# The width-96 attention's output projection as seven products of block sums

## The chip, the core and the metric

The kernel runs on one core of one Trainium2 chip. The core has a matrix engine (TensorE, PE in the profile, with its weight loads on a row of their own, PEld), a vector engine (VectorE, DVE), a scalar engine (ScalarE, ACT), a general engine (GpSimd, POOL) and a queue engine from which this kernel issues all its DMAs (SyncE, SP). The metric is the time of one execution on the device in microseconds, and the time of a kernel is the median of its runs. Less is better.

## What is computed

A decoder of four layers on 1024 tokens (16 sequences of 64) of width 512. Each layer is a cross-attention over 64 context tokens per sequence and a feed-forward part, and both add their result to the stream `x`. The change touches layer 2's second part and layer 3:

```
# layer 2, second part: 64 experts of rank 16, gated by a top-16 router
h   = einsum('nd,krd->nkr', xf, A)
out = einsum('nkr,kdr->nd', h * G[:, :, None], B) * 2
# layer 3: 16 query heads in 4 groups, width 96; one key head for each group
q, k, v = latents @ Wq.T, hidden @ Wk.T, hidden @ Wv.T
out = softmax(q k / sqrt(96)) v          # 16 heads of 96: 1536 wide
x = x + out @ Wo.T                       # Wo: 1536 -> 512, in float32
# then a linear layer with 3-bit weights, and the end
```

## The kernel before

**Two lanes.** All tokens are 8 tiles of 128. From layer 1's second part on, the work is split into two lanes of 4 tiles each: lane b ("side", tiles 0 to 3) and lane a ("main", tiles 4 to 7). Each lane is a Python generator that traces instructions and yields a cost after each step; `merged` takes from the side lane as much cost as the main lane has just yielded, times a rate. That sets the order of TensorE's instructions, which is kept as written (`manual_schedule` for PE). The instructions of the other engines and of the DMA queue are ordered by the framework's scheduler from their readiness in its own simulation, and each queue then runs strictly in that order. When lane b's work ends, lane a goes on alone.

**Memory of weights.** Each lane has four pages of 128 x 2048 floats for weights (`Lane.page`). A page is handed to the next tile as soon as its last reader is done; a load that needs a page waits for that in the DMA queue.

**Products of block sums.** The expert layer (`lora_experts`) already multiplies two 2 x 2 block matrices with seven block products in place of eight (class `Seven`): `hidden` for the first factor, `output` for the second. The sums of the activations' blocks are made by GpSimd (`stream_sums`, `hidden_sums`), those of the weights' blocks once by GpSimd in `block_sums`, which runs beside lane b's layer-2 attention: for each of 8 parts of the weights it loads 512 KB, does four subtractions of 128x256 and stores 512 KB to device memory. Each part is then loaded by both lanes as 384 KB of blocks and 512 KB of sums (`LoraWeights.load`). `block_sums` advances by one step at each yield of lane b's layer-2 attention. Parts 0 to 3 of the expert layer lie in the lane's four pages, 4 and 5 in room of their own in the layer's pool, and 6 and 7 in the pages that come free after the first `hidden` half.

**Layer-3 attention** (`packed_attention`) has 8 units in a lane, (group, pair of tiles), in the order group by group. A software pipeline runs, in each iteration n, `keys` of unit n, `turn_weights` of unit n-2, `scores` of n-1, `queries` of n, `project_both` of n-3 and `values` of n-2. For a unit, `project_both` multiplies each of its two tiles by the group's rows of Wo: three chunks of 128 rows, 512 columns wide (`Attention.project`, line 746), and VectorE adds the result to `x` (line 159). The group's query and key weights and its rows of Wo take a page each (lines 1600 and 1601). After the last unit come the norms, the transposes and the products of the last linear layer (`Q3Linear`, line 1549).

A float32 product of the code stands as two records of TensorE in the profile: 4 groups x 4 pairs of tiles x 2 tiles x 3 chunks are 96 products, and the profile has x192.

Of the kernel before, what the change touches and what calls it, by code (L numbers as in the profile page):

```python
# [1290 lines left out]
class LoraWeights:  # L1291
# [5 lines left out]
    def load(self, n, room=None):  # L1297
        if n in self.parts:
            return
        w = self.ln.page("w_l2f", 7 * W2) if room is None else room  # L1300
        half = 3 * W2
        self.ln.nc.sync.dma_start(w[:, :half], self.src[n, :, :half])
        self.ln.nc.sync.dma_start(w[:, half:], self.kept[n])
        self.parts[n] = w


def lora_experts(ln, tiles, weights, w_r):


# [4 lines left out]
    with ExitStack() as es:  # L1314
# [3 lines left out]
        for n in range(4, 6):  # L1318
            weights.load(n, pool.tile([P, 7 * W2], F32, tag=f"w{n}", name="w_l2f", bufs=1))
# [38 lines left out]
        def stream_sums(p):  # L1358
            t, u = pairs[p]
            blocks = [k.kvT[:, c : c + 2, v, 1:3, :] for v in (t, u) for c in (0, 2)]  # L1360
            a11, a12, a21, a22 = blocks
            s = pool.tile([P, 4, 2, 2, S], F32, tag="s", name="sx", bufs=1)
            nc.gpsimd.tensor_tensor(s[:, 0], a21, a22, ALU.add)
            nc.gpsimd.tensor_tensor(s[:, 1], s[:, 0], a11, ALU.subtract)
            nc.gpsimd.tensor_tensor(s[:, 2], a11, a21, ALU.subtract)
            nc.gpsimd.tensor_tensor(s[:, 3], a12, s[:, 1], ALU.subtract)
            lhs[p] = {
                f"s{i + 1}": (lambda e, i=i: s[:, i, e].rearrange("p b s -> p (b s)"))
                for i in range(4)
            }  # L1370
            lhs[p]["a11"] = lambda e: k.stream(e, t)
            lhs[p]["a12"] = lambda e: k.stream(2 + e, t)
            lhs[p]["a22"] = lambda e: k.stream(2 + e, u)
# [64 lines left out]
        def output(p):  # L1438
            x = [k.x[v].rearrange("p (j n) -> p j n", j=2) for v in pairs[p]]

            def add(v, j, src):
                nc.vector.scalar_tensor_tensor(
                    x[v][:, j], src, SCALING, x[v][:, j], ALU.mult, ALU.add
                )

            m = Seven(ln, lhs.pop(p), [weights.parts[4 + e] for e in range(4)], "ps_o")
            s = pool.tile([P, 2, W2], F32, tag="u", name="uo")
            p1, p2 = m.products(2)
            nc.scalar.copy(s[:, 0], p1)
            add(0, 0, p1)  # L1450
            add(0, 0, p2)
            yield 3.45
            p6, p7 = m.products(2)
            nc.vector.tensor_tensor(s[:, 1], s[:, 0], p6, ALU.add)
            nc.vector.tensor_tensor(s[:, 0], s[:, 1], p7, ALU.add)
            yield 3.45
            p5, p4 = m.products(2)
            nc.vector.tensor_tensor(s[:, 1], s[:, 1], p5, ALU.add)
            add(1, 1, p5)
            add(1, 0, p4)  # L1460
            add(0, 1, s[:, 1])
            add(1, 1, s[:, 0])
            add(1, 0, s[:, 0])
            yield 3.45
            (p3,) = m.products(1)
            add(0, 1, p3)
            yield 1.7
# [15 lines left out]
        for n in range(6, 8):  # L1483
            weights.load(n)
        yield from turn(0, 1)
        hidden_sums(0)
        yield from hidden(1, 1)
        out = output(0)
        yield next(out)
        yield next(out)  # L1490
        yield from turn(1, 0)
        yield from turn(1, 1)
        hidden_sums(1)
        yield from out
# [3 lines left out]
class Q3Linear:  # L1498
# [6 lines left out]
    def load(self):  # L1505
        nc, ln = self.ln.nc, self.ln
        w_q, w_ranges, bias = self.src
        self.q3 = ln.page("w_l3f", NC * D).bitcast(I32)
        nc.sync.dma_start(self.q3, w_q)

        r = ln.page("r_l3f", NC * D).bitcast(F16)
        for g in range(4):
            nc.sync.dma_start(
                r[32 * g : 32 * (g + 1)], w_ranges[g].partition_broadcast(32)
            )
        self.r = r.rearrange("p (c j n) -> p c j n", c=NC, j=2)
        self.bias = self.pool.tile([P, D], F16, tag="b16", name="b16", bufs=1)
        nc.sync.dma_start(self.bias, bias.partition_broadcast(P))
        self.wT = ln.page("wT_l3f", NC * D).rearrange("p (c n) -> p c n", c=NC)
        self.kept = {}  # L1520

    def weights(self, c):
        nc = self.ln.nc
        w, low, high = self.wT[:, c, :], self.r[:, c, 0, :], self.r[:, c, 1, :]
        nc.vector.tensor_tensor(w, high, low, ALU.subtract)
        nc.vector.scalar_tensor_tensor(
            w, self.q3[:, c * D : (c + 1) * D], 1.0 / 7.0, w, ALU.mult, ALU.mult
        )
        nc.vector.tensor_tensor(w, w, low, ALU.add)
# [14 lines left out]
    def product(self, t):  # L1544
        ln, nc = self.ln, self.ln.nc
        xT = self.kept.pop(t)
        ps = ln.bank([P, D], "ps_o")
        for c in range(NC):
            nc.tensor.matmul(
                ps, lhsT=xT[:, c, :], rhs=self.wT[:, c, :], start=c == 0, stop=c == NC - 1  # L1550
            )
        ln.add_to(t, ps)
        nc.sync.dma_start(self.out[t * P : (t + 1) * P, :], ln.k.x[t])


def packed_attention(ln, tiles, w_in, w_v, last):
# [6 lines left out]
    with ExitStack() as es:  # L1563
# [31 lines left out]
        def head_weights(h):  # L1595
            if h < NKV and h not in heads:
                n_q, n_k = NC * G * HD, NC * P
                n = n_q + (n_k if h < NJ else 0)
                wa, wb = ln.page(f"l3a_w{h}", n), ln.page(f"l3a_o{h}", NJ * D)
                nc.sync.dma_start(wa, w_in[h, :, :n])  # L1600
                nc.sync.dma_start(wb, w_in[h, :, n_q + n_k :])
                heads[h] = (
                    wa[:, :n_q].rearrange("p (c n) -> p c n", c=NC),
                    wa[:, n_q:].rearrange("p (c n) -> p c n", c=NC) if h < NJ else None,
                    wb.rearrange("p (g n) -> p g n", g=NJ),
                )

        def keys(u):
            h, t = u
            if t == tiles[0]:  # L1610
                head_weights(h)
                head_weights(h + 1)
# [50 lines left out]
        def values(u):  # L1663
            h, t = u
            d = kept[u]
            aP = pool.tile([P, NJ, 4, S], F32, tag="aP", name="aP")
# [11 lines left out]
        def project(u, i):  # L1678
            h, t = u
            aP = kept[u]["aP"]  # L1680
            chunks = [
                aP[:, j, 2 * i : 2 * i + 2, :].rearrange("p b s -> p (b s)") for j in range(NJ)
            ]
            at.project(t + i, chunks, heads[h][2])

        def project_both(u):
            for i in range(2):
                project(u, i)

        linear = Q3Linear(ln, pool, *last)  # L1690
        units = [(h, t) for h in range(NKV) for t in tiles[::2]]
        for n in range(len(units) + 2):
            for lag, step, cost in [
# [4 lines left out]
                (3, project_both, 5.2),  # L1698
                (2, values, 1.7),
            ]:  # L1700
                if n == len(units) + 1 and step == project_both:

                    for c in range(2):
                        linear.weights(c)
                        yield 1.0
                if 0 <= n - lag < len(units):
                    own = step(units[n - lag])
                    yield cost if own is None else own
            if n == len(units):
                linear.load()  # L1710
# [8 lines left out]
        project(units[-1], 0)  # L1719
        yield 2.6  # L1720
        linear.norm(three)
        linear.turn(one)
        yield 0.5
        project(units[-1], 1)
        yield 2.6
        linear.norm(four)
        linear.turn(two)
        yield 0.5
        for t, ahead in zip(tiles, (three, four, None, None)):
            linear.product(t)  # L1730
            yield 3.4
            if ahead is not None:
                linear.turn(ahead)
                yield 0.5
# [44 lines left out]
def decoder_kernel(ctx: ExitStack, tc: tile.TileContext, i: dict, out: bass.AP):  # L1779
# [7 lines left out]
    kept_s = [kept.tile([P, 4 * W2], F32, tag=f"s{n}", name=f"sums_d{n}") for n in range(8)]  # L1787
# [46 lines left out]
    def last_layers(ln, tiles, weights):  # L1834
        yield from lora_experts(ln, tiles, weights, routers[0])
        yield from packed_attention(
            ln, tiles, i["l3a_w"], i["l3a_v"], [i["l3f_q"], i["l3f_r"], i["l3f_b"], out]
        )

    def side():  # L1840
# [7 lines left out]
        with ExitStack() as es:  # L1848
            sums = block_sums(b, b.pool(es, "sums"), i["l2f_w"], kept_s)
            weights = LoraWeights(b, i["l2f_w"], kept_s)  # L1850
            for cost in small_head_attention(b, halves[0], i["l2a_w"], weights):
                next(sums, None)
# [5 lines left out]
    def main():  # L1858
# [7 lines left out]
        weights = LoraWeights(a, i["l2f_w"], kept_s)  # L1866
# [10 lines left out]
def laid_out(a):  # L1877
# [63 lines left out]
    i["l2f_w"] = np.stack(parts + [blocks(w_b, e) for e in range(4)])  # L1941
    w = [a[f"L3_xattn_W{n}"].T for n in "qkvo"]
    i["l3a_w"] = per_head(w[0], w[1], None, w[3], 96, 4)
# [25 lines left out]
```

## Time and profile before

| | |
|---|---|
| time, median of 3 runs | 1618.26 us (1617.16 to 1623.63) |
| the profiled execution: time | 1624.97 us |
| its span, first to last instruction | 1622.9 us |
| mean granted TensorE clock | 0.989 |
| lane b's layer-2 attention | about 860 to 1040 us |
| lane b's expert layer and layer 3 | about 1040 to 1473 us |
| lane a's expert layer | about 1300 to 1411 us |
| lane a's layer 3 | about 1411 us to the end, alone from about 1473 us |
| the layer-3 Wo products (line 746, `l3a_o`) | 192 records, 85.5 us |
| GpSimd's sums of weight blocks (line 1252) | 32 instructions, 22.9 us |

How to read the profile: a table of busy time by engine comes first, then the span in 40 slices, then the chain of work that ended last, followed back from the last instruction. Rows of the chain are start, length, engine, tile written, line and number of records. In the groups of instructions a row is: line, engine, operation, tile written <- tiles read, shape, number; then the busy time in us and the mean length of one in ns; then the idle time of the engine ahead of them and what ended it. The mean length of a matmul record holds its latency, which overlaps the next one; the distance between the starts of neighbours is what a record costs.

### The profile page before, as it was taken

What the parts mean: (1) busy time and instruction counts of PE and PEld (TensorE: products, weight loads), DVE (VectorE), ACT (ScalarE), POOL (GpSimd) and SP (SyncE); (2) the same over time, 40 slices, a digit from 0 to 9 for tenths busy, and PEclk for the clock granted to TensorE, in tenths of its full rate; (3) what the DMA queues carried; (4) which work ended last, traced back from release to release, by engine and by line L of the source; (5) the groups of instructions that cost most, each with busy time, mean ns of one, the idle gap of its engine ahead of it and who ended that gap; (6) DMA issues with size and microseconds to landing.
All of it is one profiled execution on the core that took longest, in us unless ns stands there. A gap on an engine that the chain in (4) does not pass through costs nothing.

```text
span 1622.9 us, 21530 instructions
## 1 busy us (share of the span) xinstructions
PE 1564.4 (96%) x7291; PEld 950.1 (59%) x7296; DVE 994.2 (61%) x2084; ACT 621.5 (38%) x1944; POOL 578.4 (36%) x614
## 2 busy tenths in 40 slices
PE   7899899999999999999999999999999999999999
PEld 1234456465555645666665565667566578757774
DVE  6687587666687566777954465449345454622335
ACT  3333444244433444444443354321234433223442
POOL 2394237532286313853324433224122132111112
PEclk9999999999999999999999999999999999999999
DMA  8892349623695345944435622214220113201120
GB/s 233 269 288 88 115 145 266 193 83 102 191 271 159 108 142 168 272 156 176 170 129 206 230 76 92 79 46 179 72 69 21 36 73 128 64 26 46 39 72 26
DMA packets 104237, 215.06 MB, mean 133 GB/s; under 512 B 49600, under 2 KB 66752, under 8 KB 93504
## 3 DMA queue, kind: packets, MB, share of 16 engines
q1 hardware_dynamic: 104128, 213.68, 41.8%
q8 instruction: 59, 0.97, 0.2%
q14 instruction: 50, 0.41, 0.1%
HBM read 190.06 MB, written 23.59 MB: 132 GB/s over the span
## 4 chain that ended last, share of the span: by engine, by line
PE 77%; DVE 12%; DMA 4%; ACT 3%; POOL 2%; issue 2%; SPq 0%; ACTq 0%; POOLq 0%; DVEq 0%
PE ps_wo L746 15%; PE ps_q L860 10%; PE ps_kv L878 5%; PE ps_q L1636 5%; PE ps_ckv L812 5%; PE ps_a L737 4%; PE ps_s L696 4%; PE ps_pT L143 3%; PE ps_o L1279 3%; DMA att<-att_d 3%; PE ps_h L1279 3%; PE ps_v L1583 3%; PE ps_k L1620 3%; PE ps_wo L1206 2%; PE ps_q L1138 2%
## 5 line engine op out<-in xcount | busy, mean ns | idle before, releaser
L746 PE MATMUL ps_wo<-l1a_o,aT 128*128 128x512 f32 x512 | 233.6, 599 | 3.1 <-ACT aT L930 3.1
L860 PE MATMUL ps_q<-l1a_w,kvT 128*128 128x512 f32 x512 | 233.0, 598 | 0.0
L712 ACT ACTIVATE p<-ps_s,mx 128x128 f32<-128x128 f32 x384 | 135.4, 369 | 221.1 <-DVE mx L707 204.9
L721 POOL TENSOR_TENSOR p<-p,sm 128x512 f32<-128x512 f32 x96 | 103.7, 1081 | 301.2 <-DVE sm L720 270.5
L125 POOL TENSOR_TENSOR r<-r,mhalf 128x5 f32<-128x5 f32 (+1 forms) x96 | 101.9, 1062 | 222.6 <-DVE r L802 219.4
L860 PEld LDWEIGHTS ps_q<-l1a_w,kvT 128*128 128x128 f32 x512 | 96.3, 192 | 116.7 <-issue 115.2
L746 PEld LDWEIGHTS ps_wo<-l1a_o,aT 128*128 128x128 f32 x512 | 93.6, 192 | 101.5 <-issue 96.8
L159 DVE TENSOR_TENSOR x<-x,ps_wo 128x512 f32<-128x512 f32 x104 | 70.6, 679 | 112.5 <-PE ps_wo L746 78.4
L878 PE MATMUL ps_kv<-l1a_w,kvT 128*128 128x256 f32 x512 | 122.7, 383 | 2.7 <-DVE x L159 2.7
L478 POOL TENSOR_TENSOR acc<-acc,pv 128x512 f32<-128x512 f32 x96 | 121.5, 1291 | 4.4 <-DVE pv L468 3.7
L812 PE MATMUL ps_ckv<-l1a_kv,kvT 128*64 128x512 f32 x512 | 116.9, 598 | 4.4 <-ACT ckv L821 4.4
L801 DVE TENSOR_REDUCE r<-sq 128x5 f32<-128x640 f32 x64 | 52.3, 817 | 103.7 <-ACT sq L886 103.7
L878 PEld LDWEIGHTS ps_kv<-l1a_w,kvT 128*128 128x128 f32 x512 | 92.7, 191 | 19.1 <-DVE x L159 4.3
L868 ACT ACTIVATE sq<-ps_q 128x512 f32<-128x512 f32 x64 | 38.2, 598 | 151.4 <-PE ps_q L860 151.4
L468 DVE TENSOR_TENSOR pv<-att,ps_v 128x512 f32<-128x512 f32 x128 | 82.1, 677 | 22.4 <-DMA att<-att_d 17.8
L125 POOL TENSOR_TENSOR rs<-rs,mhalf 128x1 f32<-128x1 f32 x64 | 37.7, 595 | 162.4 <-DVE rs L134 157.9
L696 PE MATMUL ps_s<-kT,qT 128*128 128x128 f32 (+1 forms) x704 | 91.5, 275 | 0.0
L371 DVE TENSOR_TENSOR prod<-qs,kp 128x1024 f32<-128x1024 f32 x64 | 80.9, 1301 | 14.5 <-ACT qs L352 7.6
L696 PEld LDWEIGHTS ps_s<-kT,qT 128*128 128x128 f32 (+1 forms) x704 | 85.1, 192 | 2.3 <-issue 0.9
L1636 PE MATMUL ps_q<-kvT,l3a_w 128*128 128x256 f32 x384 | 85.5, 379 | 0.0
L746 PE MATMUL ps_wo<-l3a_o,aP 128*128 128x512 f32 x192 | 85.5, 593 | 0.0
L728 DVE COPY pT<-ps_pT 128x512 f32<-128x512 f32 x96 | 64.3, 682 | 31.3 <-PE ps_pT L143 31.1
(216 smaller groups left out, 2856.2 us busy)
## 6 DMA issues: line engine op xcount, KB each, us to landing
l1a_w<-in_l1a_w SPq DMA_DIRECT2D x32, 1536.0 KB, 7.3
att<-att_d SPq DMA_DIRECT2D x64, 512.0 KB, 9.3
l1a_o<-in_l1a_w SPq DMA_DIRECT2D x32, 1024.0 KB, 5.2
s<-ckv SPq DMA_DIRECT2D x32, 256.0 KB, 4.5
w_l2f<-sums_d SPq DMA_DIRECT2D x16, 512.0 KB, 5.5
w_l2f<-in_l2f_w SPq DMA_DIRECT2D x16, 384.0 KB, 4.3
l3a_w<-in_l3a_w SPq DMA_DIRECT2D x6, 1024.0 KB, 6.5
l3a_o<-in_l3a_w SPq DMA_DIRECT2D x8, 768.0 KB, 4.3
```

Of the source, the lines that this page charges most:

```text
L125: self.nc.gpsimd.tensor_tensor(out, v, self.k.mhalf[:, : v.shape[1]], ALU.pow)
L468: nc.vector.tensor_tensor(pv.rearrange("p (q w n) -> p q w n", w=2, n=L), att[:, a, :].rearrange("p (q w n) -> p q w n", w=2, n=L), spaced ...
L478: nc.gpsimd.tensor_tensor(sums, before, pv, ALU.add)
L696: nc.tensor.matmul(ps[:, i, :], lhsT=qT[:, i // 2, 2 * (i % 2) : 2 * (i % 2) + 2, :].rearrange("p g s -> p (g s)"), rhs=kTs[i // 2], start ...
L712: nc.scalar.activation(p[:, i, :], ps[:, i, :], AF.Exp, bias=mx[:, i : i + 1], scale=self.scale, accum_out=sm[:, i : i + 1],)
L721: nc.gpsimd.tensor_tensor(p, p, bc(sm, 2, P), ALU.mult)
L746: self.nc.tensor.matmul(ps, lhsT=a, rhs=wo[:, g, :], start=g == 0, stop=g == len(chunks) - 1)
L812: nc.tensor.matmul(ps[j * S : (j + 1) * S], lhsT=k.context(c, 2 * t + 1 - j), rhs=w_pair[hp][:, c, :], start=c == 0, stop=c == NC - 1,)
L860: nc.tensor.matmul(ps, lhsT=k.stream(c, t), rhs=w_qkv[n][0][:, c, :], start=c == 0, stop=c == NC - 1,)
L878: nc.tensor.matmul(ps, lhsT=k.stream(c, t), rhs=w_qkv[n][1][:, c, :], start=c == 0, stop=c == NC - 1,)
L1279: self.ln.nc.tensor.matmul(ps[:, i % 2], lhsT=a(e), rhs=w[:, b * W2 : (b + 1) * W2], start=e == 0, stop=e == len(self.rhs) - 1,)
L1636: nc.tensor.matmul(ps[:, j], lhsT=wq[:, c, (j0 + j) * P : (j0 + j + 1) * P], rhs=k.kvT[:, c, t : t + 2, 1:3, :], start=c == 0, stop=c == N ...
```

## The change

1. In layer 3 the units of a lane are ordered so that the two groups of a pair (0 and 1, then 2 and 3) follow each other on the same two tiles. Their outputs (2 groups x 3 chunks deep) on two tiles are a 2 x 2 block matrix; so are six chunks of Wo's rows by two halves of 256 columns. They are multiplied in seven block products, in two steps of the pipeline: four products in one iteration, three in the next. GpSimd makes the activations' sums (`sums`), and the adds to `x` are those of the expert layer, moved to a function of their own (`add_seven`).
2. In lane a, the last pair of groups on the last pair of tiles (`single`) is multiplied as before, but in two halves of 256 columns.
3. `block_sums` makes sums for 14 parts instead of 8 (six parts of Wo), and advances at four of five yields of lane b's layer-2 attention; what is left of it then is traced at that layer's end.
4. Layer 3 gets Wo in three parts for each pair of groups: two in pages, one in a room of one buffer; the second pair's are traced at the end of iteration 7.
5. Lane a's expert layer has no room of its own for parts 4 and 5: its parts 4 to 7 are loaded into pages as these come free, and its order of work is changed.
6. The last linear layer's weights and bias lie in buffers of the attention.

```
+def add_seven(ln, m, s, x, factor, cost):
...
+    p1, p2 = m.products(2)
+    nc.scalar.copy(s[:, 0], p1)
+    add(0, 0, p1)
+    add(0, 0, p2)
+    yield cost
+    p6, p7 = m.products(2)
+    nc.vector.tensor_tensor(s[:, 1], s[:, 0], p6, ALU.add)
+    nc.vector.tensor_tensor(s[:, 0], s[:, 1], p7, ALU.add)
+    yield cost
+    p5, p4 = m.products(2)
+    nc.vector.tensor_tensor(s[:, 1], s[:, 1], p5, ALU.add)
+    add(1, 1, p5)
+    add(1, 0, p4)
+    add(0, 1, s[:, 1])
+    add(1, 1, s[:, 0])
+    add(1, 0, s[:, 0])
+    yield cost
+    (p3,) = m.products(1)
+    add(0, 1, p3)
+    yield cost / 2
...
 def lora_experts(...):
...
+        if more_room:
+            for n in range(4, 6):
+                weights.load(
+                    n, pool.tile([P, 7 * W2], F32, tag=f"w{n}", name="w_sums", bufs=1)
+                )
...
-        for n in range(6, 8):
+        later = range(6 if more_room else 4, 8)
+        yield from turn(0, 1)
+        for n in later[:2]:
             weights.load(n)
-        yield from turn(0, 1)
         hidden_sums(0)
         yield from hidden(1, 1)
...
+        else:
+            for n in later[2:]:
+                weights.load(n)
+            yield 3.0
+            yield from turn(1, 0)
+            yield 3.0
+            yield from turn(1, 1)
+            hidden_sums(1)
+            yield 2.0
+            yield from output(0)
         yield from output(1)
...
 def packed_attention(...):
...
+        def out_weights(hp):
+            first = 8 + NJ * hp
+            whole = alone and hp == 1
+            for n in range(first, first + 2):
+                w_out.load(n, whole=whole)
+            room = late.tile([P, (8 if alone else 7) * W2], F32, tag="o", name="w_sums", bufs=1)
+            w_out.load(first + 2, room, whole)
...
+        def sums(u):
+            h, t = u
+            if h % 2 and u not in single:
+                one, two = kept.pop((h - 1, t))["aP"], kept.pop(u)["aP"]
+                a11, a12, a21, a22 = (v[:, :, 2 * i : 2 * i + 2] for i in range(2) for v in (one, two))
+                s = late.tile([P, 3, NJ, 2, S], F32, tag="sa", name="sa", bufs=1)
+                nc.gpsimd.tensor_tensor(s[:, 1], a11, a21, ALU.subtract)
+                nc.gpsimd.tensor_tensor(a21, a21, a22, ALU.add)
+                nc.gpsimd.tensor_tensor(s[:, 0], a21, a11, ALU.subtract)
+                nc.gpsimd.tensor_tensor(s[:, 2], a12, s[:, 0], ALU.subtract)
...
+        def project_half(u):
+            if u in single:
+                cost = sum(running.pop()) if running else 0.0
+                for i in range(2):
+                    project_one(u, i)
+                return cost + 5.2
+            if u[0] % 2:
+                running.append(project(u))
+                return next(running[0]) + next(running[0])
+            if running:
+                return sum(running.pop())
+            return 0.0
...
-        units = [(h, t) for h in range(NKV) for t in tiles[::2]]
+        units = [(2 * p + j, t) for p in range(NKV // 2) for t in tiles[::2] for j in range(2)]
...
+        single = units[-2:] if alone else []
...
-                (3, project_both, 5.2),
+                (3, project_half, 5.2),
                 (2, values, 1.7),
+                (2, sums, 0.0),
...
+            if n in (1, 7):
+                late = late or ln.pool(es, "l3b")
+                out_weights(n // 7)
...
-            for cost in small_head_attention(b, halves[0], i["l2a_w"], weights):
-                next(sums, None)
+            for n, cost in enumerate(small_head_attention(b, halves[0], i["l2a_w"], weights)):
+                if n % 5 < 4:
+                    next(sums, None)
                 yield cost
```

## The prediction

> **What bounds the kernel now.** I read the table of engines first, then the shares of the chain, then the chain in order of time where lane a runs alone, then the windows of the stages that change.
>
> ```profile
> PE 1564.4 (96%) x7291; PEld 950.1 (59%) x7296; DVE 994.2 (61%) x2084; ACT 621.5 (38%) x1944; POOL 578.4 (36%) x614
> PE 77%; DVE 12%; DMA 4%; ACT 3%; POOL 2%; issue 2%; SPq 0%; ACTq 0%; POOLq 0%; DVEq 0%
> ```
>
> TensorE is busy in 96% of the span and makes 77% of the chain. One iteration of layer 3 in lane a, as the chain has it:
>
> ```profile
> 1520.21 5.18 PE ps_q L1636 x24
> 1525.39 5.15 PE ps_wo L746 x12
> 1530.54 1.73 PE ps_a L737 x8
> 1532.27 3.43 PE ps_k L1620 x8
> 1535.70 0.87 PE ps_pT L143 x8
> 1536.58 1.79 PE ps_s L696 x16
> 1538.36 5.18 PE ps_q L1636 x24
> ```
>
> Each piece ends where the next starts: no wait in between. These rows also give prices: a 512-wide record costs 5.15 / 12 = 0.429 us, a 256-wide one 5.18 / 24 = 0.216 us. The windows (columns: length, then busy us and instructions of PE, PEld, DVE, ACT, POOL, then clock, DMA share, GB/s):
>
> ```profile
> 850.00:875.00 25.00, 23.95 (x93) 13.38 (x95) 12.82 (x31) 8.61 (x29) 11.94 (x16) 1.00 0.42 148
> 875.00:900.00 25.00, 24.32 (x121) 15.93 (x120) 8.28 (x19) 9.60 (x29) 12.39 (x17) 1.00 0.88 311
> 900.00:925.00 25.00, 25.00 (x150) 14.64 (x149) 8.60 (x17) 7.90 (x23) 10.45 (x13) 1.00 0.61 218
> 1200.00:1300.00 100.00, 95.17 (x622) 61.94 (x621) 55.60 (x122) 48.50 (x144) 26.95 (x28) 0.98 0.12 40
> 1300.00:1475.00 175.00, 173.35 (x760) 125.03 (x759) 77.40 (x206) 49.61 (x162) 37.80 (x48) 1.00 0.19 68
> 1475.00:1600.00 125.00, 124.89 (x548) 86.65 (x547) 52.22 (x110) 56.48 (x223) 18.08 (x18) 1.00 0.15 45
> ```
>
> From 1300 us on PE stands still for under 2 us in 300, while DVE, ACT and POOL are below half. Here TensorE's work is the time, and a microsecond less of it is one off the end, if nothing new makes PE wait.
>
> **The change part by part.**
>
> *TensorE's products (the gain).* Two groups on a pair of tiles are 2 x 2 x 3 = 12 products of 512 columns, 24 records: 24 x 0.429 = 10.30 us. Seven block products of 3 chunks and 256 columns are 42 records: 42 x 0.216 = 9.07 us (1.23 to 1.24 less by the unrounded pieces). There are 2 pairs of groups x 2 pairs of tiles x 2 lanes = 8 such blocks; 7 change: -8.65 us. The last block becomes 48 records of 256 columns, 10.36 us: +0.06. Sum **-8.6 us**. It assumes that a record of 256 columns keeps its 0.216 us: `ps_q` has them so, with a new weight load for each record, 190 ns by its row and thus shorter than the product beside it.
>
> ```profile
> L1636 PEld LDWEIGHTS ps_q<-kvT,l3a_w 128*128 128x128 f32 x384 | 72.0, 190 | 10.2 <-issue 1.0
> ```
>
> A rule speaks against this. The Trainium skill, page "TensorE: Matmul & The Clock Gate", section "Back-to-back issue gap", says that in a stream of weight loads and products both set the pace, with about 81 ns for 128 columns and 131 ns for 512. Read linearly between, 256 columns would cost some 98 ns, three quarters of 512 (an estimate from that page); seven narrow products would then cost 42 x 0.75 x 0.429 = 13.5 us a block, and the sum of the seven would be +22 us. This trace has one half, not three quarters, and I go by the trace.
>
> *Vector and scalar adds.* A block had 4 adds of 128x512 (line 159, 0.679 us each: 2.7 us); it gets 11 of 128x256 (lines 1389 and 1442, 0.416 us: 4.6 us) and one copy on ACT (line 1391, 0.37 us). That is +1.9 us of DVE a block, +13 us in all, beside products: DVE is busy 52 of 125 us where lane a is alone. I count 0. Without that cover a bank of PSUM would come free late, but four other allocations of the lane stand between, over 5 us of products.
>
> *GpSimd's sums of activations.* Four instructions of 128x384 a block. The trace has 128x256 at 0.73 us (line 1363) and 128x512 at 1.29 us (line 1424), so about 1.0 us each, 4 us a block, 28 us in all. The wait is new: PE's third product (s2) waits for the third of them, and behind it in PE's order stand both lanes. In most iterations keys, transposes, scores and queries lie between `values` and `project_half`: 3.43 + 0.87 + 1.79 + 5.18 = 11.3 us, against 1.9 us until ACT has copied `aP` after `values` (4 copies for each tile, 0.47 + 3 x 0.25 us) and 3 us of sums. In iteration 8 there are no keys and queries: 0.87 + 1.79 us and the first two products (2.6 us) make 5.3 us against 4.9 us and the semaphores between. I take +0.5 us, bounds 0 and 4 (all four sums in the open).
>
> On shared ports: at 1599.7 us one DVE instruction of line 1526 took 1.53 us beside a GpSimd one of 1.60 us; others of its line took 0.68. The Trainium skill, page "SBUF — State Buffer", section "SBUF: two separate sides", calls it an exclusive lock for DVE instructions with two SBUF inputs. By it, three adds of a block could each be held up by up to one sum; DVE has the room for that, as above.
>
> *GpSimd's sums of weights, and their DMAs.*
>
> ```profile
> L1252 POOL TENSOR_TENSOR sums<-sums 128x256 f32<-128x256 f32 x32 | 22.9, 738 | 20.3 <-DMA sums<-in_l2f_w 19.7
> ```
>
> Eight parts took 22.9 us and made POOL wait 19.7 us for their loads. Six more: 24 x 0.738 = 17.7 us of POOL, about 14.8 us of such waits, 6 loads and 6 stores of 512 KB on SP's queue at about 0.35 us an issue. Queued behind them on POOL are lane a's norm factors (line 125) and softmax factors (line 721), on SP lane a's keys, values and weights of layer 1. Upper bound, all in the open: 32.5 us; lower 0. The nearest row is the stage that already has eight: PE stood 1.05 + 0.68 + 0 us in the windows from 850 to 925 us, 1.73 us in all. Per part 0.22 us, for six **+1.3 us**. The slower pace moves steps later; counting yields, 47 of 57 steps come before lane b's attention ends, and ten (7.4 us of POOL) after.
>
> *Weights of layer 3.* Wo comes in 12 loads of 896 KB to 1 MB for 8 of 768 KB; with pieces, SP gets 27 issues for 8. All but the second room are far ahead of use. The second room (part 13) waits for the last product of the first pair's rest in iteration 7, and PE needs it after `values`, transposes and scores: 1.73 + 0.87 + 1.79 = 4.4 us, plus two chunks of the first product, 0.86. Its first piece should land 3.2 us after release, its second after 5 us (two such pieces at 1162 us landed 3.2 and 5.0 us after the first was issued), and the third product needs that at 7.9 us. I count 0.
>
> *Lane a's expert layer without room.* Parts 6 and 7 now wait for the end of `hidden(1, 1)`; four pieces issued together at 1347.9 us had all landed 7.3 us later. `output(0)` is put off by 0.9 + 3.0 + 0.9 + 3.0 + 0.9 + 2.0 = 10.7 us of side work and 1.75 us of transposes, 12.5 us: 0. The values' weights of lane a (`l3a_wv`) lay ready since 1365 us and now wait for `output(1)`, whose last product releases its first page 1.3 us before it ends; the load took 4.8 us, so it lands 3.5 us after the end. PE began with them 4.3 us after (1414.64 against 1410.36 us). 0, with 0.8 us to spare. The landings' spread for the parts was wide:
>
> ```profile
> DMA to landing us min/median/max: 3.1/4.9/13.1
> ```
>
> *A possible gain.* A lane's first Wo products come an iteration later, out of the windows from 1200 to 1300 us, where PE loses 4.8 us, partly to a busy DVE. I take 0, down to -2.
>
> **Sum:** -8.6 + 0.5 + 1.3 = -6.8 us. For the profiled execution (1622.9 us span, 1624.97 us time) that is 1618.2. It ran 6.7 us above the median; I assume that this extra stays as it is, and put the difference on the median: 1618.26 - 6.8 = **1611.5 us**.
>
> **Rivals.**
>
> *The gain is eaten by waits (0.20).* The new sums of weights hold POOL and SP beside layer 1's attention of lane a at more than 0.22 us a part, because they now run into lane b's softmax, where POOL's line 1175 works too. At 1.3 us a part (a sixth of its POOL time and waits) the six cost 8 us: about 1618. For it: a 5 us wait of POOL for a load delays whatever is behind. Against it: PE lost almost nothing there, and lane a has several us between factor and use.
>
> *Late loads: slower (0.12).* Three loads now follow a release shortly before use: parts 6 and 7, `l3a_wv`, part 13. If they land like the slowest row, 13.1 us, PE waits 13.1 - 12.5 = 0.6, 13.1 - 1.3 - 4.3 = 7.5 and 13.1 - 5.2 = 7.9 us: 16 us, and the sum is +9.2: 1627.5. Against it: the slow row stands in a burst of eleven loads between 1097 and 1107 us. It makes the kernel slower than before once the three exceed their cover by 6.8 us in sum.
>
> *The products don't get cheaper (0.08).* If the narrow records with operands made by GpSimd cost 24 x 0.429 / 42 = 0.245 us, the gain is gone: with the waits 1620.
>
> **How the numbers follow.** The forecast has 0.60, from 1606.6 (-10.6 and the runs' 1.1 us below their median) to 1614.5. The range 1606.5 to 1622 leaves out the slower rival and edges of the others. The measurement can tell about 0.5%, 8.1 us, from no change: faster means below 1610.2, slower above 1626.4. About half of the forecast's cases lie below 1610.2, where the waits come to nothing: faster 0.30. The other half and two rivals lie within: 0.57. Slower 0.13.
>
> **What the profile after would show.** Right: pieces of `ps_wo` of 0.216 us a record (342 records for 192), PE busy without gaps after 1475 us, lane b's layer-2 stage with at most 2 to 3 us of idle PE, layer 3 of lane a starting with no wait for `l3a_wv`. Wrong: waits of PE for POOL `sa`, for the parts' DMAs, or for line 125 or 721 behind line 1252; records of `ps_wo` well above 0.216 us.

## The result, and the profile after

| | before | after |
|---|---|---|
| median of eight runs each, us (lowest to highest) | 1617.34 (1614.92 to 1623.63) | 1626.99 (1622.45 to 1633.77) |
| profiled execution: time / span, us | 1624.97 / 1622.9 | 1622.45 / 1620.6 |

The ratio is 1.0056 with a 95% interval from 1.003 to 1.0081: the change made the kernel slower by about 9 us, where 6.8 us less were forecast. The two profiled executions must not be compared whole: that of before ran 6.7 us above the median of the three runs first made, that of after is the fastest of its own eight. The first 860 us, which no edit touches, took 6.8 us less after than before. From there on the changed kernel is the slower one in the profiles too.

The table of engines and the shares of the chain after:

```profile
PE 1556.8 (96%) x7441; PEld 980.8 (61%) x7446; DVE 1012.3 (62%) x2133; ACT 623.9 (38%) x1951; POOL 631.0 (39%) x666
PE 71%; DVE 14%; DMA 5%; POOL 4%; ACT 3%; issue 3%; SPq 1%; DVEq 0%; ACTq 0%; POOLq 0%
```

TensorE is busy 7.6 us less, and still its share of the chain fell from 77% to 71%, while that of POOL doubled. The windows of after, with the columns of the prediction:

```profile
850.00:925.00 75.00, 71.31 (x347) 42.67 (x348) 27.88 (x58) 26.46 (x81) 41.20 (x54) 1.00 0.62 218
925.00:1050.00 125.00, 119.86 (x704) 73.63 (x705) 69.16 (x159) 54.85 (x162) 46.05 (x50) 0.97 0.37 132
1300.00:1475.00 175.00, 168.93 (x773) 132.00 (x772) 82.06 (x222) 45.78 (x144) 48.66 (x58) 0.99 0.25 88
1475.00:1600.00 125.00, 124.79 (x632) 102.41 (x631) 58.67 (x132) 58.26 (x227) 33.60 (x31) 1.00 0.19 59
```

The stretch from 850 to 925 us had 73.3 us of busy PE before (the sum of three windows in the prediction) and has 71.3 now, and the granted clock falls to 0.97 after it. From 1300 to 1475 us 1.7 us of idle PE have become 6.1. From 1475 us on nothing is wrong.

**The products are as cheap as forecast.** Two pieces of the chain in lane a's layer 3:

```profile
1521.28 5.18 PE ps_wo L1279 x24
1536.33 3.88 PE ps_wo L1279 x18
```

24 + 18 records in 9.06 us are 0.216 us each.

**The first loss stands in lane b's attention of layer 2**, where the sums of weights run on GpSimd. PE's waits from 850 to 1060 us (us in total, times, longest); these three head the list and are new, the others are those of before:

```profile
PE ps_pT L143 <- DVE p L1170: 2.3, 1, 2.3
PE ps_qT L143 <- DVE qn L901: 2.1, 1, 2.1
PE ps_kv L878 <- DVE x L159: 1.1, 1, 1.1
```

DVE is named, but it was waiting itself. Here are GpSimd, DVE and PE in order of time around the second of these waits (start, us, the instructions, and in brackets the idle time before them and what ended it):

```profile
917.29 5.74 POOL L1252 TENSOR_TENSOR sums<-sums 128x256 f32<-128x256 f32 x8 [4.85 <-DMA sums<-in_sums_w]
922.99 1.17 POOL L125 TENSOR_TENSOR r<-r,mhalf 128x5 f32<-128x5 f32 x1
```

```profile
913.78 0.17 DVE L802 TENSOR_SCALAR r<-r 128x5 f32<-128x5 f32 x1
...
924.19 0.69 DVE L901 TENSOR_TENSOR qn<-qn,r 128x512 f32<-128x512 f32 x1 [6.08 <-POOL r L125]
```

```profile
925.03 0.63 PE L143 MATMUL ps_qT<-ident,qn 128*128 128x128 f32 x4 [2.06 <-DVE qn L901]
```

GpSimd takes its instructions in order. What lane a's norm factor `r` (line 125) is made from was there at 913.95 us (DVE's line 802). GpSimd stood before a sum whose load had not landed, 4.85 us in all and 3.3 us of them after that moment, then did eight sums in 5.7 us, and only then computed `r`, 9.0 us after its input. Before, at the same place, `r` had followed its input at once:

```profile
920.81 1.17 POOL L125 TENSOR_TENSOR r<-r,mhalf 128x5 f32<-128x5 f32 x1 [4.15 <-DVE r L802]
```

In the changed kernel DVE waited 6.08 us for `r`, with lane b's softmax queued behind `qn`, and PE waited for both lanes. The load and the sums that begin the chain are two engines away from the wait that the table names.

**The clock makes it dearer.** In the stretch behind this wait, and in one behind a wait at lane b's end, the granted clock (the column after POOL's) was half:

```profile
925.80:932.60 6.80, 5.68 (x13) 4.10 (x14) 5.36 (x13) 3.57 (x10) 3.04 (x3) 0.50 0.95 345
1413.90:1417.30 3.40, 3.40 (x9) 2.71 (x9) 0.14 (x1) 0.00 (x0) 0.00 (x0) 0.50 0.00 0
```

PE looks busy in them, but does half the work: 2.8 and 1.7 us lost (half of its 5.68 and 3.40 busy us). The first stretch and the new waits, 2.8 + 2.3 + 2.1 + 1.1 us, are 8.3 of the 9.1 us that this stage lost. The Trainium skill, page "TensorE: Matmul & The Clock Gate", section "What's actually happening", has the clock fall to half after an idle window of about 3.4 us. Here less was enough: PE had stood still for 2.06 us when the clock fell at 925.8 us (its second gap, 1.15 us, lies inside the stretch of half clock), so the rule is no safe bound in this trace.

The traces show more. Every stretch of half clock in the thirteen profiles is 3.41 us long or a multiple of that (only the last one is cut short by the end), and within a profile all begin and end on one grid of this step. What counts is how much idle time of PE falls into one step. In the changed kernel a wait of 2.54 us at lane b's end puts 3.41 - 1.17 = 2.24 us into one step, and half clock follows. In the kernel of the fourth experiment the same wait, 2.55 us, is split over two steps, 1.37 and 1.18 us, and full clock follows (first the changed kernel's step, then three of the other's):

```profile
1410.50:1413.91 3.41, 1.17 (x5) 1.06 (x6) 1.57 (x5) 0.11 (x1) 3.18 (x4) 1.00 0.00 0
```

```profile
1406.86:1410.28 3.42, 2.05 (x10) 1.47 (x8) 3.39 (x11) 0.37 (x1) 3.31 (x4) 1.00 0.00 0
1410.28:1413.69 3.41, 2.23 (x10) 2.00 (x11) 0.51 (x2) 0.00 (x0) 2.12 (x3) 1.00 0.00 0
1413.69:1417.10 3.41, 2.44 (x12) 1.80 (x12) 1.86 (x5) 0.00 (x0) 0.00 (x0) 1.00 0.38 119
```

Counted over all thirteen profiles from 30 us on, half clock followed every one of 69 steps at full clock with 1.91 us or more of idle PE, none of 5741 steps with less than 1.28 us, and 14 of the 111 between.

**The second loss is spread over layer 3**, between 1300 us and the end:

```profile
PE ps_wo L1279 <- POOL sa L1718: 2.5, 1, 2.5
PE ps_o L1576 <- ACT xT L1568: 1.5, 2, 0.7
PE ps_xT L143 <- DVE xn L136: 1.0, 1, 1.0
PE ps_v L1610 <- ACT kvT L178: 0.8, 1, 0.8
```

Before, the list for this stretch was:

```profile
PE ps_r L1332 <- ACT kvT L178: 1.0, 1, 1.0
PE ps_v L1583 <- ACT kvT L178: 0.7, 1, 0.7
```

Why `sa` is late, GpSimd in order of time shows:

```profile
1399.15 1.20 POOL L1716 TENSOR_TENSOR sa<-aP 128x384 f32<-128x384 f32 x1 [2.08 <-PE ps_wo L1279]
1404.73 0.55 POOL L125 TENSOR_TENSOR rs<-rs,mhalf 128x1 f32<-128x1 f32 x1 [4.39 <-DVE rs L134]
...
1409.37 1.00 POOL L1717 TENSOR_TENSOR aP<-aP 128x384 f32<-128x384 f32 x1
1410.33 1.40 POOL L125 TENSOR_TENSOR rs<-rs,mhalf 128x1 f32<-128x1 f32 x2
1411.70 0.99 POOL L1718 TENSOR_TENSOR sa<-aP 128x384 f32<-128x384 f32 x1
```

The four sums of lane b's last pair are 1.0 to 1.2 us each, about as forecast, but between the first and the second stand norm factors and bias adds of the linear layer, and a 4.39 us wait for DVE. This pair's sums are needed behind the loop, where the linear layer's work has begun; the forecast had looked at iteration 8, and at nothing that GpSimd does in between.

**The account.** From PE's starts I worked out how much longer each record's step to the next took than the median step of its kind, and summed this excess by stage. The mark is lane b's first product with the keys' weights of layer 2; all before it is untouched (but for one experiment). Microseconds of the profiled execution:

| kernel | start to mark | mark to end | PE's plain work | excess, lane b layer 2 | excess, lane a experts, lane b's end | excess, lane a layer 3 | excess, rest |
|---|---|---|---|---|---|---|---|
| before | 867.1 | 755.8 | 710.2 | 14.1 | 0.8 | 1.2 | 29.5 |
| after | 860.3 | 760.3 | 701.7 | 23.2 | 7.2 | 3.5 | 24.7 |

From mark to end: -8.5 (products) + 9.1 + 6.4 + 2.3 - 4.8 = +4.5 us. Of the rest's 4.8 us most is scatter: a kernel with the old products (the first experiment) had 25.9 there, and 10.2 us at half clock fell into it before, 3.4 us after. Without the rest the sum is +9.3 us, near the 9.7 us between the medians.

### The profile page after: what moved, and what is told of

Same layout as the page of the kernel before. It is cut to its first block, busy times and chain, and to the rows that moved or that the text cites. A ratio compares the mean times of both kernels' runs of the same rounds, so it can differ in the third digit from the quotient of the medians.

```text
span 1620.6 us, 21994 instructions
## 1 busy us (share of the span) xinstructions
PE 1556.8 (96%) x7441; PEld 980.8 (61%) x7446; DVE 1012.3 (62%) x2133; ACT 623.9 (38%) x1951; POOL 631.0 (39%) x666
## 4 chain that ended last, share of the span: by engine, by line
PE 71%; DVE 14%; DMA 5%; POOL 4%; ACT 3%; issue 3%; SPq 1%; DVEq 0%; ACTq 0%; POOLq 0%
PE ps_wo L746 9%; PE ps_q L860 9%; PE ps_q L1668 5%; PE ps_kv L878 5%; PE ps_ckv L812 5%; PE ps_s L696 4%; PE ps_wo L1279 4%; PE ps_a L737 4%; PE ps_pT L143 3%; PE ps_k L1652 3%; PE ps_v L1610 3%; PE ps_h L1279 2%; DMA att<-att_d 2%; PE ps_wo L1206 2%; PE ps_o L1576 2%
## 5 line engine op out<-in xcount | busy, mean ns | idle before, releaser
L159 DVE TENSOR_TENSOR x<-x,ps_wo 128x512 f32<-128x512 f32 x76 | 51.4, 676 | 58.2 <-PE ps_wo L1206 35.1
L712 ACT ACTIVATION_READ_ACCUMULATOR p<-ps_s,mx 128x1 f32 x384 | 79.6, 207 | 0.0
```

The lines of the kernel that those rows point to most:

```text
L712: nc.scalar.activation(p[:, i, :], ps[:, i, :], AF.Exp, bias=mx[:, i : i + 1], scale=self.scale, accum_out=sm[:, i : i + 1],)
```

## The experiments

Theory: GpSimd, standing in its order before loads and norm steps, holds up PE twice, and takes back more than the products give. Rivals: the products themselves, SP's queue, or GpSimd's busy time are the price. All were timed in 5 rounds beside the kernel before on the same chip (first four, next four and last three on one chip each).

**1. The sums of weights alone.** The kernel before, with its Wo, gets all 14 parts of sums at the changed kernel's pace:

```
-            sums = block_sums(b, b.pool(es, "sums"), i["l2f_w"], kept_s)
+            sums = block_sums(b, b.pool(es, "sums"), i["sums_w"], kept_s)
...
-                next(sums, None)
+                if n % 5 < 4:
+                    next(sums, None)
```

> The kernel before with one part of the change alone: GpSimd makes the sums of 14 parts of weights at the change's pace, but layer 3 multiplies by Wo as before and never reads the six new parts. Theory 1 (GpSimd's six more parts cost the time, in lane b's layer-2 attention): that stage grows by about 9 us, as in the changed kernel (186.2 for 177.1 us there), and the time by 8 to 12 us, to about 1627. Rival, theory 2 (the cost is in layer 3: sums of activations and late loads): the stage grows by 1 to 2 us and the time by no more.

Ratio 1.0073 (1.0048 to 1.0099), 11.8 us more in the medians, as the first theory expected. The stage's excess is 23.2 us as in the changed kernel, with the same waits and 6.8 us of half clock:

```profile
PE ps_pT L143 <- DVE p L1170: 2.3, 1, 2.3
PE ps_qT L143 <- DVE qn L901: 2.2, 1, 2.2
...
```

So the six parts by themselves make the first loss; the new products have no share in it.

**2. Without them.** The changed kernel computes only the eight old parts; for Wo it loads the plain blocks in the sums' place, so the sums of Wo's blocks are left out of the computation.

```
+        sums = self.kept[n] if n < 8 else self.src[n]
+        self.ln.nc.sync.dma_start(w[:, some:all_], sums)
...
+            sums = block_sums(b, b.pool(es, "sums"), i["sums_w"][0:8], kept_s)
```

> The changed kernel without the six new parts' sums: GpSimd makes 8 parts as before, and where layer 3 reads the other six it loads plain blocks of the same size, so the sums of Wo's blocks are left out of the computation. Theory 1: lane b's layer-2 attention falls back to about 177 us and the time to 1615 to 1618. Rival, theory 2: the time stays at 1625 or more.

Ratio 0.997 (0.9954 to 0.9986), 1616.17 us, as the first theory expected. The stage is back at an excess of 14.1 us, and layer 3 keeps its waits. GpSimd's row for the sums from 855 to 1050 us (busy, mean ns, idle before and what ended it), first of the changed kernel, then of this one:

```profile
L1252 POOL TENSOR_TENSOR sums<-sums 128x256 f32<-128x256 f32 x56 | 40.4, 746 | 32.6 <-DMA sums<-in_sums_w 31.6
```

```profile
L1252 POOL TENSOR_TENSOR sums<-sums 128x256 f32<-128x256 f32 x32 | 23.2, 748 | 18.4 <-DMA sums<-in_sums_w 17.8
```

The six parts cost GpSimd 17.2 us of work and 13.8 us of waiting for loads. What of this PE pays for, the fourth and the seventh experiment bear on.

**3. The last pair's activation sums on VectorE.**

```
+                eng = nc.vector if u == units[-1] else nc.gpsimd
-                nc.gpsimd.tensor_tensor(s[:, 1], a11, a21, ALU.subtract)
+                eng.tensor_tensor(s[:, 1], a11, a21, ALU.subtract)
...
```

> The changed kernel with the activations' sums of lane b's last pair made by VectorE instead of GpSimd, where they stood behind norm factors and bias adds in GpSimd's order. Theory 2: the wait of 2.5 us for sa at 1410 us is gone and with it 3.4 us of half clock (worth 1.7 us): 4 us less than the changed kernel, about 1623. Theory 1 alone: within 2 us of the changed kernel's 1627.

Ratio 1.004 (1.002 to 1.006). The wait for `sa` is gone from the list, with 0.4 us for DVE `rs` in its place, and the excess of that stage fell from 7.2 to 3.8 us. The time, 1.6 parts in 1000 under the changed kernel's, has an interval that overlaps with it, and its median, 1627.12 us, is not the 1623 expected: the wait is shown in the trace, its worth in the time is not resolved.

**4. Loads three ahead.** The sums are written over their own operands, so a room of 8 KB a partition becomes 4 KB, and four rooms stand where two stood. The work is the same.

```
-            rooms[n] = pool.tile([P, 2, 4 * W2], F32, tag="room", name="sums")
+            rooms[n] = pool.tile([P, 4 * W2], F32, tag="room", name="sums", bufs=bufs)
...
-    load(0)
+    for n in range(bufs - 1):
+        load(n)
...
+                ((b11, b12, b11), (b12, b22, b12), (b22, b22, b11), (b21, b21, b22))
...
-                    load(n + 1)
+                    load(n + bufs - 1)
```

> The changed kernel with the weights' sums made in place, in four rooms of half the size instead of two: three parts are loaded ahead, so GpSimd should no longer stand waiting for loads; the number of sums is the same. If theory 1 holds and the price is that wait with the work queued behind it, the stage falls from 186 to 178 us or less and the time by 6 to 9 us, to 1618 to 1621. If the price is GpSimd's busy time (24 x 0.73 us), the stage stays above 184 us and the time within 2 us of 1627.

Ratio 0.9971 (0.9952 to 0.999): the changed kernel's loss is gone. The same row:

```profile
L1254 POOL TENSOR_TENSOR sums<-sums 128x256 f32<-128x256 f32 x56 | 41.3, 743 | 12.7 <-DMA sums<-in_sums_w 9.5
```

Busy time is the same, 41.3 against 40.4 us; the wait for loads is 9.5 us instead of 31.6. The stage's excess fell from 23.2 to 16.6 us, and the list of PE's waits there has none for `qn` and `p`; one of 1.6 us for ACT's `qn` (line 870) is left, which the later kernels with these rooms don't all have. So the price is no fixed one for GpSimd's work: over the 14.1 us of excess with eight parts, the same 56 sums cost PE 9.1 us with loads one part ahead and 2.5 us with loads three ahead. GpSimd ran up to 12 sums (9.72 us) in one go ahead of a softmax step here, and that cost PE nothing that shows.

That PE pays for the standing still alone is not shown. Of the 9.0 us by which `r` came late in the changed kernel, 5.7 were sums. With the earlier loads the last sum starts at 923.4 us instead of 950.1, so that only four of the sums, not 24, run beside lane b's softmax (from 919.5 us here, from 915.0 in the changed kernel); less waiting and an earlier end come together in this run. Nor was SP's queue tested by itself: it issues as many loads and stores as before, but in another order.

The stage took 179.6 us, more than the 178 expected, the time a little less than the 1618 to 1621. By the ratios this kernel lies 13.7 us under the changed one, by the profiles from mark to end 7.1 us. Part of what is between them is the clock: its mean over the runs was 0.9912 here and 0.9876 in the changed kernel, which over 1620 us is about 5.5 us (an estimate from these two figures; the two were not timed side by side).

**5. Both mends together** (the third edit on the fourth kernel).

> The four rooms of e4, and the last pair's sums of activations on VectorE as in e3. If the two costs are separate, PE's wait of 2.5 to 2.7 us for sa near 1409 us is gone and the time lies 2 to 4 us below that of the four rooms alone: a ratio of 0.995 to the kernel before. If what is gained there is given back at lane a's start of layer 3, the ratio stays at 0.997.

Ratio 0.9973 (0.9962 to 0.9985). In its profile it is 3.5 us shorter than the fourth from mark to end, 2.3 of it at lane b's end; in the time the two can't be told apart. A miss for the expected gain.

**6. More cover at two places, on the fifth.** Lane a's first value products wait for `l3a_wv` and for `xn`, lane b's linear tail for `xT`. A larger count of work at the first yield lets the planner put more of lane b in between, and the tail turns tiles two ahead from the start.

```
-        yield 2.5
+        yield 5.0 if alone else 2.5
...
-            ahead = (None, three, four, None)
+            ahead = (three, four, None, None)
```

> As e5, and lane a's layer 3 begins after 5.0 instead of 2.5 of the side lane's work, so that the load of l3a_wv, which now starts only at the end of output(1), lies beside more products; lane b's last linear layer turns its tiles two products ahead again, as in the kernel before. Waits of 1.1 us for l3a_wv, 1.0 us for the norm before it and twice 0.9 us for xT should go: 2 to 4 us below e5, a ratio of 0.993. If the side lane's work is only moved and not added as cover, the waits come back at its end and the time is that of e5.

Ratio 0.9923 (0.9904 to 0.9941), the fastest kernel of the study: 1610.36 us, 13 us less than before on that chip. By the ratios that is 8 us less than the fifth, where 2 to 4 were expected; by the profiles 4.9 us from mark to end, 2.3 of them in lane b's layer 2, which this edit does not touch. From 1300 us on PE's list of waits is this:

```profile
PE ps_wo L1281 <- DVE rs L134: 0.4, 1, 0.4
PE ps_h L1281 <- POOL sx L1406: 0.3, 1, 0.3
PE ps_wo L1281 <- DMA w_sums<-in_sums_w: 0.3, 1, 0.3
PE ps_v L1612 <- ACT kvT L178: 0.2, 1, 0.2
```

**7. The sums a stage earlier** (the fourth kernel, half the pace, begun beside lane b's mxfp4 layer).

```
+            for cost in mxfp4_ffn(b, halves[0], i["l1f_w"], i["l1f_b"], kept_w):
+                next(sums, None)
+                yield cost
...
-                if n % 5 < 4:
+                if n % 2:
```

> As e4, but the sums of weights begin a stage earlier, beside lane b's quantised layer, and go at about half the pace. If what is left of their cost (179.6 against 177.1 us in lane b's layer-2 attention) is GpSimd's busy time in that stage, it falls to 177 us and the time by 2 us, unless the stage before (80.7 us, VectorE nearly full) grows by as much.

Ratio 1.0098 (1.008 to 1.0116). Lane b's layer 2 is back at an excess of 14.1 us, but the stage before it grew by 22.2 us: from PE's `ps_mx` at 776 us to the mark it took 106.4 us, in the changed kernel 84.2. PE's waits there, from 760 to 890 us:

```profile
PE ps_qT L143 <- DVE qn L901: 13.2, 2, 9.0
...
```

It is the same victim, lane a's `qn`. GpSimd and DVE at the longest of these waits:

```profile
773.69 10.45 POOL L1254 TENSOR_TENSOR sums<-sums 128x256 f32<-128x256 f32 x13
784.10 1.17 POOL L125 TENSOR_TENSOR r<-r,mhalf 128x5 f32<-128x5 f32 x1
```

```profile
785.30 0.69 DVE L901 TENSOR_TENSOR qn<-qn,r 128x512 f32<-128x512 f32 x1 [9.73 <-POOL r L125]
```

GpSimd waits for no load in this row: thirteen sums stand ahead of `r`, and PE waits 9.0 us. So GpSimd's work, too, is paid for where it stands ahead of `r`. That this stage is worse ground is shown; which of GpSimd's neighbours there makes it so was not tried.

**8. No pacing** (the changed kernel with a step of sums at every yield).

```
-                if n % 5 < 4:
-                    next(sums, None)
+                next(sums, None)
```

> The changed kernel without the pace: one step of the weights' sums at each yield of lane b's layer-2 attention. If the pace spares anything, the stage grows beyond the changed kernel's 186 us and the time beyond 1.006 of the kernel before. If GpSimd's order follows the loads and not the place in the trace, as the sums' times before suggest (done at 917 us, far ahead of their place), the stage stays within 2 us.

Ratio 1.003 (1.0013 to 1.0047); the profiled stage had an excess of 26.3 us, and the last sum starts at 955.2 us, against 950.1 with the pace. Its time is not above the changed kernel's, so the pace spares nothing that can be measured.

**9 to 11. What the sixth kernel's gain is made of**, each on the fourth kernel: the longer pause alone, the tail's order alone, and both with the activation sums left on GpSimd. The edits are those shown under 6.

> Four rooms for the weights' sums, with 2.5 us more of lane b's work counted between lane a's norm factors and its first layer-3 products; the tail's order and the place of the activation sums stay as in the changed kernel. Theory (the gain of the version with everything came from the waits it takes away): the wait of TensorE for l3a_wv (about 0.8 to 1.2 us) and for xn (about 1 us) go, those for sa (2.5 us) and xT (1.5 us) stay; against the version with four rooms alone 1 to 2 us less, ratio to before about 0.996. Rival (the gain came mostly from one place, where a wait also lowered the granted clock): if it is this one, 5 us or more less, ratio 0.993 to 0.994.

> Four rooms, and lane b's linear tail turned two tiles ahead from the start; the pause before layer 3 of lane a and the place of the activation sums stay. Theory (sum of waits): the two waits for xT (1.5 us) go, those for l3a_wv, xn and sa stay; 1 to 2 us less than with four rooms alone, ratio to before about 0.996. Rival (one place): if it is this one, 5 us or more less, ratio 0.993 to 0.994.

> Four rooms, the longer pause and the tail turned two ahead, with the last pair's activation sums still on GpSimd. Theory (moving those sums to VectorE brought next to nothing by itself): 0.992 to 0.994, as the version with all. Rival (the 2.5 us wait for sa and the low clock behind it are part of that version's gain): 0.994 to 0.996, and the trace shows TensorE's wait for sa of about 2.5 us with a stretch of half clock behind it.

Ratios 0.9966 (0.9949 to 0.9984), 0.997 (0.9953 to 0.9987) and 0.9958 (0.9941 to 0.9976). The pause takes away the waits for `l3a_wv` and `xn` (2.1 us of excess at lane b's end), the tail's order those for `xT` (1.7 us in the last stage), and in the eleventh both are gone. No one place gives 5 us by itself, which speaks for a sum of waits. In the eleventh the wait for `sa` stands alone:

```profile
PE ps_wo L1281 <- POOL sa L1720: 2.6, 1, 2.6
```

No half clock followed it here (the granted clock is 1.00 from 1400 to 1420 us, with the wait ending at 1408.5; the wait is split 1.4 and 1.1 us over two steps of the clock's grid), so the low clock behind `sa` in the changed kernel is not a fixed part of that wait. Of the eight kernels with this wait, half clock followed in the changed one and the eighth, with 2.2 and 2.3 us of it in one step, and in none of the other six, with at most 1.9. Less 2.6 us (1.6 parts in 1000) this kernel would be at 0.9942, where the sixth has 0.9923 with an interval up to 0.9941; whether more than the wait is behind the difference stays open. Of the expectations the sum of waits held for the ninth and tenth; for the eleventh neither theory held whole: its ratio is the rival's, but without the low clock.

The account of the experiments' profiles, in the columns used above, with the ratios:

| kernel | start to mark | mark to end | plain work | lane b layer 2 | lane b's end | lane a layer 3 | rest | ratio |
|---|---|---|---|---|---|---|---|---|
| 1 sums alone | 862.4 | 761.1 | 710.0 | 23.2 | 0.8 | 1.2 | 25.9 | 1.0073 |
| 2 without them | 866.9 | 750.5 | 702.1 | 14.1 | 5.7 | 3.4 | 25.2 | 0.997 |
| 3 `sa` on DVE | 864.0 | 758.8 | 701.8 | 25.4 | 3.8 | 3.1 | 24.7 | 1.004 |
| 4 four rooms | 864.9 | 753.2 | 701.7 | 16.6 | 5.9 | 3.6 | 25.4 | 0.9971 |
| 5 both | 863.9 | 749.7 | 702.2 | 16.8 | 3.6 | 3.7 | 23.4 | 0.9973 |
| 6 and cover | 862.5 | 744.8 | 702.2 | 14.5 | 1.6 | 1.6 | 24.9 | 0.9923 |
| 7 a stage earlier | 883.2 | 750.0 | 702.1 | 14.1 | 5.6 | 3.8 | 24.4 | 1.0098 |
| 8 no pacing | 867.3 | 763.6 | 702.2 | 26.3 | 7.5 | 3.3 | 24.3 | 1.003 |
| 9 pause | 860.1 | 748.6 | 701.7 | 14.5 | 3.8 | 3.8 | 24.8 | 0.9966 |
| 10 tail | 860.7 | 752.0 | 701.7 | 17.6 | 5.8 | 1.9 | 25.0 | 0.997 |
| 11 pause, tail | 864.2 | 746.9 | 701.8 | 16.6 | 3.8 | 1.6 | 23.1 | 0.9958 |

Read it down the columns: the plain work falls by 8.0 to 8.5 us wherever Wo is changed, and by nothing else; lane b's layer 2 is at 23 us or more exactly where 14 parts run in two rooms beside it. The scatter from start to mark (860 to 867 us, without the seventh, whose edit lies ahead of the mark) is as large as what is looked for, and it is why the whole span of one profile decides nothing here.

## Why the prediction was wrong, point by point

- **TensorE's products, -8.6 us: right.** The records took 0.216 us, the plain work fell by 8.5. The rule set against it (an estimate from the Trainium skill, "TensorE: Matmul & The Clock Gate", section "Back-to-back issue gap", three quarters of a 512-wide record's time for 256 columns) would have given 0.32 us and does not hold for these records.
- **GpSimd's sums of weights, +1.3 us: the step that failed.** It measured +9.1 us in the stage. The prediction took PE's idle time per part from the stage's windows, 0.22 us, and multiplied it by six more parts. But the idle time of a stage is no price per part. In the profile of before GpSimd stood 5.02 us before a load, did eight sums and then `r` as well, at 878.71 us; DVE was busy with other work until then and waited 0.52 us:

```profile
885.82 0.69 DVE L901 TENSOR_TENSOR qn<-qn,r 128x512 f32<-128x512 f32 x1 [0.52 <-POOL r L125]
```

  In the changed kernel's later stretch the same order of work made DVE wait 6.08 us. The eight old parts end at 916.7 us in before, and DVE's first step of lane b's softmax is at 921.7; the six new ones stand beside it. That the two lanes' steps on DVE are what turns a late `r` into a late PE is read from the order of the trace; no run took them apart. The prediction also had the slower pace put ten steps behind the end of lane b's attention; the last sum starts at 950.1 us, some 96 us ahead of that end, and without the pace 5 us later. The upper bound, 32.5 us, was on the page, and the low end was chosen from windows that held no case of the mechanism.
- **The rival "the gain is eaten by waits" named this mechanism**, with GpSimd's work in lane b's softmax and a 5 us wait for a load. It was given 0.20 and priced at 8 us, which is close to the 9.1 measured for this part. (The 1.3 us a part behind the 8 are called a sixth of GpSimd's time and waits; by the prediction's own 17.7 + 14.8 us for six parts they are a quarter.) What it left out are the losses in layer 3 that come on top, and so the sign.
- **GpSimd's activation sums, +0.5 us: the size of an instruction right, the place wrong.** 2.5 us, for lane b's last pair, where norm factors and bias adds stand between the first and the second sum. The forecast compared the sums with PE's work until they are needed, and took GpSimd as free in between. In the changed kernel's profile 1.7 us of low clock followed, in the eleventh experiment's none.
- **Weights of layer 3, 0: right for the parts** (0.2 to 0.5 us), **wrong for `l3a_wv`**: 0.8 us to spare had been counted, and it came about 1 us late (0.8 to 1.2 in the experiments that show it by name). With the waits for `xn` (1.0) and `xT` (1.5), which no step had looked at, that is some 3.5 us which the sixth kernel no longer has; by the ratios it gains 8 us over the fifth, and the rest of that stays open.
- **Vector adds, 0: right.** No wait of PE for DVE's new adds shows in layer 3.
- **Lane a's first Wo products an iteration later, 0 to -2: not settled.** The rest's excess is 29.5 and 25.9 us with the old products, 23.1 to 25.4 with the new.
- **That the profile's extra time stays as it is** was harmless for the sum of differences, but it hid that a profile of this kernel varies by 7 us in stretches that nothing touches.

The range (1606.5 to 1622) missed the 1626.99 us by 5 us, since it has room for one loss of about 8 us and two came: 9.1 us in lane b's layer 2, and 6.4 + 2.3 us later.

## What to carry to other kernels

Before giving an in-order engine more work, list whose instructions stand behind each of its waits and what those hold up in turn; what GpSimd had to do ahead of a norm step, waits for loads and sums alike, was paid by PE through DVE. More rooms with earlier loads bought most of it back at the same amount of work (9.1 to 2.5 us), and the same work a stage earlier cost 22 us. Don't scale a stage's idle time by the count of what is added: look for the place where the next one lands. When spans of the same code differ by more than the effect, compare stage by stage from a mark behind the untouched part.

## What the runs showed of the hardware that was not expected

- Half clock came in stretches of 3.41 us or multiples of that, on one grid for each profile, and followed every step of the grid with 1.91 us or more of idle PE, no step with less than 1.28, and 14 of 111 between. A wait of 2.55 us was followed by half clock or by full clock according to where it lay on the grid: 2.2 and 2.3 us in one step in two kernels, at most 1.9 in six.
- A GpSimd sum of 128x256 took 0.743 us in the fourth kernel, and sums of 128x384 1.0 to 1.2 us. Work and waiting for loads grew with the count of parts: from 8 to 14 parts, 23.2 to 40.4 us of work and 17.8 to 31.6 us of waiting (the second experiment and the changed kernel). Out of proportion was what PE lost: 14.1 us of excess in the stage with 8 parts, 23.2 with 14.
